# Gate logits of the first layer: eight dot products per token tile on VectorE in place of transposes and products on TensorE

## The chip, the cores and the metric

The kernel runs on one core of one Trainium2 chip. The metric is the device time in microseconds (us) from launch to end; for each kernel the median of several runs is given, and one more run is profiled. A core has several engines that work side by side and wait for one another on semaphores: TensorE (PE in the profile, with its weight loads as PEld), VectorE (DVE), ScalarE (ACT), GpSimd (POOL) and SyncE (SP, which here only issues DMA transfers).

## The reference

Two layers run one after the other over 2708 tokens (rows) of 256 numbers. Each has a masked attention, then a layer of eight experts of which every token uses two. Cut to what matters here, and with the shapes in brackets, layer 0 is:

```python
x = x + elu(softmax(where(adj > 0, q @ k.T / 16, -9e15)) @ v)   # q, k, v from layernorm(x)
xt = layernorm(x)                                # [2708, 256]
logits = xt @ Wr + br                            # [2708, 8]: the gate
probs = softmax(logits)
top_p, top_idx = top_k(probs, 2)
weights = top_p / top_p.sum(axis=-1)
xn = (xt - mean(xt)) / sqrt(var(xt) + 1e-5)      # normed a second time
# expert e: gelu((xn * ln_g[e] + ln_b[e]) @ W1[e] + b1[e]) @ W2[e] + b2[e]
x = x + sum of the two chosen experts' outputs, by weights
```

Layer 1 has another attention and another eight experts with the same top two; the change touches only the gate of layer 0. Since `xt` is `(x - mean) * once`, where `once` is one factor per token, the logits without bias are `once` times the dot of `x` with the gate's column less that column's mean over the 256 rows.

## The kernel before, in words

**Tiles.** Tokens go in 22 tiles of 128 rows (the last has 20), a tile's rows on the 128 partitions. Queries are worked on in six blocks of 512 (the last has 148 queries, tiles 20 and 21 being its two; the 512-query blocks hold four tiles each).

**Attention of layer 0** (`layer0_attention`). Each block goes over the 22 key tiles, one key step `k` each: `scores` (L545, products of 128x512 into the PSUM tile `s`, which has two buffers), the exponential on ACT (L557), the mask on DVE (L560, a multiplication by 0 or 1), and `attend` (L609, four products into the PSUM tiles `acc`), which runs three key steps behind its scores (`LAG`). At the ends of blocks the last columns' masks come in through small products (L552, with `apart` made by DVE in L432) and comparisons (L564, L595). While block b runs, DVE builds the masks of block b+1 out of `adj` (L411, L417), into the tile `mT`; after a block its masks are written to DRAM for layer 1 (`neighbours<-mT`).

**Routing.** When a block ends, `evict` copies its `acc` to `raw` (L634) and puts one sequence of steps for each tile on a `Line`: a new tile begins every three key steps, and every key step moves each begun tile on to its next `yield`. The sequence is `finish` (L297 to L302, L617 to L628: division by the sum, elu with ACT's exponential in L622, addition of x) and then `Experts.route`:

- `norm_stats`: mean and variance (L251, L252), then factors `once` and `twice` by a power on POOL (L257);
- `xt`, the row normed once (L261, the group xn<-x), and the row normed twice (L261, row<-x), which is copied (L1143), since a row is sent to two experts;
- `to_columns`: two transposes of `xt` on PE (L274) and a copy by ACT to `gT` (L275);
- two products of `gT` with the gate `wr` (L1156, four records in the trace for a tile), and the bias added by DVE (L1160);
- top two (L1167, L1168), exponential (L1185), the choice as zeros and ones in `sel` (L1183), each row's place by two small products (L1188, L1189) and some DVE work (L1192 to L1204), and two indirect DMAs by POOL (L1207), which send the rows to `disp`.

Tiles 0 to 15 go this way in blocks 1 to 4, 16 and 17 in block 5, and 18 to 21 in the first slots of the experts that follow. In block 1, one step of `fold_gate` every four key steps prepares weights of layer 1; it begins with two dots on DVE (L212) over `wdst_b`, one of the constants loaded at the start.

**Experts of layer 0** (FFN0, `slots`). Each slot takes 128 rows of one expert: columns of the rows (L1429, L1435), up products (L1457), gelu on ACT (L1465), down products (L1473), scaling by DVE (L1479), and addition to the token's row by an indirect DMA of POOL (L1492).

**Order.** SP's transfers are issued in the order written. The instructions of the other engines are put in order by a scheduler that works on its own estimates, so a change in one place can move instructions in others; the engines then run their orders strictly. Layer 1 has orders written by hand.

Of the kernel before, what the change touches and what calls it, by code (L numbers as in the profile page):

```python
# [9 lines left out]
F32 = mybir.dt.float32  # L10
I32 = mybir.dt.int32
# [9 lines left out]
P = 128  # L21
# [83 lines left out]
def adj_ffn_kernel(ctx: ExitStack, tc: tile.TileContext, a: dict, out: bass.AP):  # L105
# [81 lines left out]
    gb_b = load_bcast("L1_ffn_gate_b", E)  # L187
    bfc_b = load_bcast("L1_gnn_b_fc", D)

    wdst_b = load_bcast("L1_gnn_w_att", D, D)  # L190

    def load_dmajor(pool, name, n):
        t = pool.tile([P, DC, n], F32, name=f"{name}_w")
        nc.sync.dma_start(t, a[name].rearrange("(c p) n -> p c n", p=P))
        return t

    wr = const.tile([P, DC, E], F32, name="wr")
    wg = const.tile([P, DC, E], F32, name="wg")


    wfc = const.tile([P, DC, VALUES + 1 + E], F32, name="wfc")

    bfc_gate = const.tile([P, E], F32, name="bfc_gate")
    for to, name in ((wr, "L0_ffn_Wr"), (wg, "L1_ffn_gate_w"), (wfc[:, :, :D], "L1_gnn_W_fc")):
        constants.append(
            partial(nc.sync.dma_start, to, a[name].rearrange("(c p) n -> p c n", p=P))
        )

    def fold_gate():
        for c in range(DC):  # L210
            junk = small.tile([P, D], F32, name="junk", bufs=1)
# [4 lines left out]
        share = routing.tile([P, DC, P], F32, name="gT", bufs=2)  # L216
# [12 lines left out]
        def times_gate(dst, src):  # L229

            turned = routing.tile([P, DC, P], F32, name="gT", bufs=2)
            to_columns(turned, src, P)
            ps = misc.tile([P, GROUP, P], F32, name="misc").rearrange("p g n -> p (g n)")
            for c in range(DC):
                nc.tensor.matmul(
                    ps[:, :E], turned[:, c], G[:, c], start=(c == 0), stop=(c == DC - 1)
                )
            nc.vector.tensor_copy(dst, ps[:, :E])

        for c in range(DC):  # L240
            times_gate(wfc[:, c, D:VALUES], wfc[:, c, :D])
            yield
        times_gate(bfc_gate, bfc_b)


    def norm_stats(src, r):

# [105 lines left out]
    def layer0_attention(line):  # L353
        with ExitStack() as scope, ExitStack() as until_last:
# [114 lines left out]
                    )  # L469
                nc.scalar.copy(v[:r, t, :D], ps[:r, :D])  # L470

            with tc.tile_pool(name="fold", bufs=1, side="right") as fold:
                wq = load_dmajor(fold, "L0_gnn_Wq", D)
                wk = load_dmajor(fold, "L0_gnn_Wk", D)
                load_x(0)
                load_x(1)
                wv = load_dmajor(wide, "L0_gnn_Wv", D)
                for t in range(2, 9):
                    load_x(t)

                with tc.manual_schedule(
                    engines={mybir.EngineType.DVE, mybir.EngineType.Pool}
                ):
                    begun = [norm_begin(t) for t in range(2)]
                    first = []
                    for t in range(2, 4):
                        first.append(norm_end(*begun.pop(0)))
                        begun.append(norm_begin(t))
                    first.extend(norm_end(*x) for x in begun)
                    mT = mask_of(0)  # L490
                    first_mask = masks_of(0, mT)
                    for _ in range(GROUP):
                        next(first_mask)
                for start in constants:
                    start()

                flat = []
                for w in (wq, wk):
                    f = fold.tile([P, DC, D], F32, name=f"flat{len(flat)}")
# [145 lines left out]
            folding = fold_gate()  # L645
            for b, (b0, nb, ts_) in enumerate(BLOCKS):
                later_mask = iter(())
                if b + 1 < len(BLOCKS):
# [2 lines left out]
                for k in range(NT):  # L651
# [384 lines left out]
        return packed, hc, w2, b2, b1, ln, row  # L1036

    class Experts:
        def __init__(self, layer, hidden, packed_weights, w_gate, gate_bias, own_norm, xd, disp, early):
            self.hidden, self.packed_weights, self.own_norm = hidden, packed_weights, own_norm  # L1040
            self.w_gate, self.gate_bias, self.xd, self.disp = w_gate, gate_bias, xd, disp

            self.seen = const.tile([P, E], BF16, name=f"seen{layer}")
            nc.vector.memset(self.seen, 0.0)
# [59 lines left out]
        def route(self, t, x, logits=None):  # L1104


            own_norm, xd, disp, seen = self.own_norm, self.xd, self.disp, self.seen
            w_gate, gate_bias = self.w_gate, self.gate_bias
            r = ROWS[t]
            if own_norm:  # L1110
                rows2 = routing.tile([P, 2, DROW], F32, name="row")
            else:
                rows2 = kept_pool.tile([P, 2, DROW], F32, name="row", bufs=6)
            mean, once, twice, _ = norm_stats(x[:r], r)
            yield
            if not own_norm:

# [2 lines left out]
                self.beside_early(nc.sync.dma_start(of_tile(xd, t), x[:r]))  # L1120

            if own_norm:
                xt = rows.tile([P, D], F32, name="xn", bufs=4)[:r]
                normed(xt, x[:r], mean, once)
                normed(by_quarters(rows2[:r, 0, :D]), in_chunks(x[:r]), mean, twice)
            else:
                row = normed(by_quarters(rows2[:r, 0, :D]), in_chunks(x[:r]), mean, once)
# [4 lines left out]
            else:  # L1132
# [7 lines left out]
                    reason="no sooner than the row",  # L1140
                )
            if own_norm:
                nc.vector.tensor_copy(rows2[:r, 1, :D], rows2[:r, 0, :D])  # L1143
            yield
            if not own_norm:
                (nc.vector.tensor_copy if self.begun else nc.scalar.copy)(
                    rows2[:r, 1, :D], rows2[:r, 0, :D]
                )
            lg = small.tile([P, E], F32, name="lg")
            if logits is None:  # L1150
                gT = routing.tile([P, DC, P], F32, name="gT", bufs=2)
                to_columns(gT[:, :, :r], xt, r)
                yield
                ps = misc.tile([P, GROUP, P], F32, name="misc").rearrange("p g n -> p (g n)")
                for c in range(DC):
                    nc.tensor.matmul(  # L1156
                        ps[:r, :E], gT[:, c, :r], w_gate[:, c, :],
                        start=(c == 0), stop=(c == DC - 1),
                    )
# [426 lines left out]
    experts0 = Experts(0, 1024, packed0, wr, br_b, True, xd0, disps[0], 16)  # L1586
    experts1 = Experts(1, 512, packed1, wg, gb_b, False, xd1, disps[1], 14)

    neighbours = [
        dram.tile([P, m.width], FP8, name=f"neighbours{b}") for b, m in enumerate(MASKS)  # L1590
# [77 lines left out]
```

## Time and profile before

| | |
|---|---|
| three runs | 1214.02, 1209.07, 1212.79 us; median 1212.79 |
| profiled execution | 1217.16 us, of which the span of the page 1215.5 |
| mean granted TensorE clock | 0.982 |
| before block 1 (0 to 112 us) | PE busy 101.0, DVE 63.1 |
| blocks 1 to 5 (112 to 501 us) | PE busy 383.9, DVE 215.5 |
| experts of layer 0 (501 to 816 us) | PE busy 313.6, DVE 87.5 |
| layer 1 and the end (816 to 1215 us) | PE busy 347.0, DVE 200.1 |

In a profile line for a group of instructions stand the source line, the engine, the operation, the tiles it writes and reads with their shapes, and a count; then the busy time in us and the mean time of one in ns; then the idle time of the engine ahead of them and what ended it. Busy times of PE overlap between records, so differences of starts are the better measure of what an instruction holds the engine. In a line of the timeline the start comes first, then the duration in us. A line of waits names who waited for whom, then the total, the number of times and the longest.

### The profile page before, as it was taken

Reading aid. Unit: us, or ns where it says so; the run is one execution under the profiler, and the core shown is the slowest. Engines: PE = TensorE matmul, PEld = TensorE weight load, DVE = VectorE, ACT = ScalarE, POOL = GpSimd, SP = SyncE. Lnnn points to the kernel's source line nnn. Section 1 sums busy time; section 2 is a strip of 40 time slices with the busy share of each in tenths; the row PEclk is TensorE's granted clock in tenths of the full one; section 3 lists DMA queues with packets and bytes.
Section 4 is the critical chain, followed back from the end, with each engine's and each line's share of the span. In section 5 each row is a group of like instructions: output and inputs, shape, how many; then the busy total and the mean of one; then the engine's idle time right before and its main releaser. Section 6 shows DMA issues by size and latency. Waiting matters only on the chain. (4 is left out here: it accounts for less than half of the span.)

```text
span 1215.5 us, 20794 instructions
## 1 busy us (share of the span) xinstructions
PE 1145.4 (94%) x6512; PEld 924.1 (76%) x6512; DVE 566.2 (47%) x2147; ACT 431.9 (36%) x1252; POOL 416.0 (34%) x519
## 2 busy tenths in 40 slices
PE   8989999999998999999999999998999988899990
PEld 5666666666665666789999999996999977789880
DVE  5466663754645647452222222224866776322224
ACT  3222221221212222353333333333776747444440
POOL 3011021110211213253333343334645558555540
PEclk9999999999998999899999999999999999999996
DMA  9394962999969394847677955633002427555557
GB/s 200 58 181 76 194 160 88 226 209 267 221 133 219 83 192 164 276 102 219 174 222 228 352 118 154 179 95 100 1 1 76 178 62 209 168 139 132 170 179 282
DMA packets 199628, 197.11 MB, mean 162 GB/s; under 512 B 91403, under 2 KB 183012, under 8 KB 193368
## 3 DMA queue, kind: packets, MB, share of 16 engines
q1 hardware_dynamic: 172442, 109.39, 40.6%
q0 software_dynamic: 26176, 83.56, 21.8%
q10 hardware_dynamic: 894, 2.77, 0.6%
q8 instruction: 54, 0.88, 0.3%
q14 instruction: 62, 0.51, 0.1%
HBM read 252.62 MB, written 66.15 MB: 262 GB/s over the span
## 5 line engine op out<-in xcount | busy, mean ns | idle before, releaser
L1457 PEld LDWEIGHTS mm<-xe,ring 128*128 128x128 f32 x2192 | 259.7, 194 | 26.0 <-issue 11.7
L1457 PE MATMUL mm<-xe,ring 128*128 128x128 f32 x2192 | 265.6, 278 | 14.5 <-DMA ring<-L_ffn_packed,weight_row 7.1
L1473 PE MATMUL acc<-ring,hT 128*128 128x256 f32 x1096 | 254.3, 381 | 1.1 <-issue 1.1
L1465 ACT ACTIVATE hT<-mm,ring 128x128 f32<-128x128 f32 x548 | 156.6, 370 | 273.1 <-issue 168.1
L1473 PEld LDWEIGHTS acc<-ring,hT 128*128 128x128 f32 x1096 | 201.3, 191 | 26.0 <-issue 2.3
L609 PEld LDWEIGHTS acc<-v,p 128*128 128x128 f32 (+1 forms) x880 | 159.7, 190 | 65.2 <-issue 41.0
L609 PE MATMUL acc<-v,p 128*128 128x257 f32 (+1 forms) x880 | 204.6, 384 | 2.3 <-DVE p L560 1.3
L545 PE MATMUL s<-g,xnT 128*128 128x512 f32 x420 | 203.0, 603 | 0.0
L1479 DVE SCALAR_TENSOR_TENSOR y<-acc,who,bias 128x256 f32<-128x256 f32 x92 | 44.4, 482 | 339.2 <-PE acc L1473 322.9
L257 POOL TENSOR_TENSOR ln_rs<-ln_rs,minus_half 128x2 f32<-128x2 f32 x88 | 66.0, 752 | 252.0 <-DVE ln_rs L253 214.4
L1207 POOL DMA_INDIRECT disp<-row,to x88 | 90.4, 1027 | 166.2 <-DVE to L1204 58.2
L1368 POOL DMA_INDIRECT ring<-L_ffn_packed,weight_row x92 | 97.6, 1060 | 128.3 <-PE acc L1473 88.4
L557 ACT ACTIVATE p<-s 128x512 f32<-128x512 f32 x105 | 62.5, 596 | 181.4 <-PE s L545 143.0
L854 PE MATMUL acc<-parts,m 128*128 128x266 f32 x924 | 126.2, 293 | 0.0
L854 PEld LDWEIGHTS acc<-parts,m 128*128 128x128 f32 x924 | 117.1, 185 | 4.1 <-ACT raw L881 0.9
L545 PEld LDWEIGHTS s<-g,xnT 128*128 128x128 f32 x420 | 76.6, 192 | 53.8 <-issue 50.5
L560 DVE SCALAR_TENSOR_TENSOR p<-p,mT 128x512 f32<-128x512 f32 x100 | 68.4, 686 | 95.2 <-ACT p L557 93.6
L1492 POOL DMA_INDIRECT xd<-y,who x45 | 71.8, 1595 | 118.7 <-issue 70.4
L821 ACT CAST m<-mT 128x512 fp32r<-128x512 fp8e4 (+4 forms) x168 | 71.6, 475 | 11.4 <-PE acc L854 7.0
L1485 POOL DMA_INDIRECT xd<-y,who x47 | 47.1, 1002 | 23.6 <-issue 11.0
L411 DVE TENSOR_SCALAR m_rows<-adj 128x512 fp8e4<-128x512 int32 (+1 forms) x105 | 42.1, 432 | 2.0 <-DMA adj<-in_adj_dram 1.9
L417 DVE STREAM_TRANSPOSE mT<-m_rows 128x128 int32<-128x128 int32 x100 | 33.4, 393 | 0.1
(252 smaller groups left out, 1028.3 us busy)
## 6 DMA issues: line engine op xcount, KB each, us to landing
adj<-in_adj_dram SPq DMA_DIRECT2D x100, 256.0 KB
L_ffn_packed<-in_L_ffn_W_dram SPq DMA_DIRECT2D x16, 1024.0 KB
xg<-disp SPq DMA_DIRECT2D x368, 32.0 KB
L_ffn_packed<-in_L_ffn_W_dram SPq DMA_DIRECT2D x16, 512.0 KB
neighbours<-mT SPq DMA_DIRECT2D x5, 1408.0 KB
mT<-neighbours SPq DMA_DIRECT2D x5, 1408.0 KB
xin<-in_x_dram SPq DMA_DIRECT2D x42, 128.0 KB
ring<-L_ffn_packed SPq DMA_DIRECT2D x4, 1154.0 KB
```

The source lines that it names most:

```text
L257: nc.gpsimd.tensor_tensor(rs[:r, 1], rs[:r, 0], minus_half[:r], ALU.pow)
L545: nc.tensor.matmul(ps[:kr, :nb], xnT[:, c, k0 : k0 + kr], g[:, c, :nb], start=(c == 0), stop=(c == DC - 1 and k < KEYS),)
L560: nc.vector.scalar_tensor_tensor(p, p, LARGEST, mask, op0=ALU.min, op1=ALU.mult)
L609: nc.tensor.matmul(accs[j][:r], p[keys, q0 : q0 + r], v[keys, k, :], start=(k == 0), stop=(k == NT - 1),)
L821: nc.scalar.copy(m[:, : q1 - q0], MASKS[b].of_key(mTs[b], k)[:, q0 - b * BN : q1 - b * BN],)
L854: nc.tensor.matmul(acc[:r], masks[t], parts[:, k, i], start=(k == 0 and i == 0), stop=False,)
L1207: nc.gpsimd.indirect_dma_start(disp[:], bass.IndirectOffsetOnAxis(ap=to[:r, j : j + 1], axis=0), rows2[:r, j], None,)
L1368: nc.gpsimd.indirect_dma_start(w, None, packed[:], bass.IndirectOffsetOnAxis(ap=self.weight_row[:, s : s + 1], axis=0), bounds_check=E * P ...
L1457: nc.tensor.matmul(ps[:, i, :], w[:, c * hidden + f * P : c * hidden + (f + 1) * P], xe[:, c, :], start=(c == 0), stop=(c == DC - 1),)
L1465: nc.scalar.activation(hT[:, f, :], ps[:, i, :], AF.Gelu, bias=w[:, b1 + f : b1 + f + 1])
L1473: nc.tensor.matmul(ps, hT[:, f, :], w[:, w2 + f * D : w2 + (f + 1) * D], start=(f == 0), stop=(f == hc - 1),)
L1492: start = nc.gpsimd.indirect_dma_start(xd[:], at, y, None, bounds_check=N - 1, oob_is_err=False, compute_op=ALU.add)
```

## The change

For layer 0 the row `xt`, its transposes, the copy to `gT`, the products and the addition of the bias out of PSUM are gone. In their place stand eight multiplications with accumulation on DVE for a tile (`gate_dots`), each of which leaves one logit per token: four behind the statistics and four behind the copied row. They read the row before normalisation, and `wr_rows`, which holds the eight gate columns, less their means, as rows on all 128 partitions. The elementwise products are written to the second half of the tile `rows2` and are overwritten by the copied row. The factor `once` and the bias are then applied in one instruction. `wr_rows` is made at the end of block 0 (`gate_rows`): a broadcast load into a buffer of `adj`, a sum on DVE, and a subtraction on POOL. One `yield` in `route` goes, since there is no product to wait for.

Some tiles move as well: `wr` is gone; `wdst_b` is loaded in `fold_gate` at the beginning of block 1 and no longer at the start; it, `junk` and `gT` of `fold_gate` come from the pool `wide`; and the weights of the first stage lie in a buffer of `mT`. The small writes of padding rows to `disp` are issued by SP two row fetches earlier.

```diff
-    wdst_b = load_bcast("L1_gnn_w_att", D, D)
...
-    wr = const.tile([P, DC, E], F32, name="wr")
+    wr_rows = rows0.tile([P, E, D], F32, name="wr_rows", bufs=1)
...
-    def fold_gate():
+    def fold_gate(pool):
+        wdst_b = pool.tile([P, D], F32, name="wdst_b", bufs=1)
+        nc.sync.dma_start(wdst_b, a["L1_gnn_w_att"][D : 2 * D].partition_broadcast(P))
...
+    def gate_rows(raw):
+
+        raw = raw.rearrange("p (d e) -> p d e", e=E)
+        mean = small.tile([P, E], F32, name="gate_mean", bufs=1)
+        nc.vector.tensor_reduce(mean, raw.rearrange("p d e -> p e d"), AX.X, ALU.add)
+        nc.vector.tensor_scalar(mean, mean, 1.0 / D, None, ALU.mult)
+        nc.gpsimd.tensor_tensor(
+            wr_rows, raw.rearrange("p d e -> p e d"),
+            mean.unsqueeze(2).to_broadcast([P, E, D]), ALU.subtract,
+        )
+
+    def gate_dots(lg, x, r, experts, unused):
+
+        for e in experts:
+            nc.vector.scalar_tensor_tensor(
+                unused, x, 1.0, wr_rows[:r, e],
+                op0=ALU.mult, op1=ALU.mult, accum_out=lg[:r, e : e + 1],
+            )
...
+                    if b == 0 and k == NT - 4:
+                        raw = wide.tile([P, BN // QUARTER, P], I32, name="adj", bufs=3)
+                        raw = raw.rearrange("p n e -> p (n e)").bitcast(F32)
+                        nc.sync.dma_start(
+                            raw, a["L0_ffn_Wr"].rearrange("d e -> (d e)").partition_broadcast(P)
+                        )
+                        gate_rows(raw)
...
             mean, once, twice, _ = norm_stats(x[:r], r)
+            lg = small.tile([P, E], F32, name="lg")
+            if own_norm:
+                dots = small.tile([P, E], F32, name="dots")
+                gate_dots(dots, x[:r], r, range(E // 2), rows2[:r, 1, :D])
+                logits = dots[:r]
             yield
...
             if own_norm:
-                xt = rows.tile([P, D], F32, name="xn", bufs=4)[:r]
-                normed(xt, x[:r], mean, once)
                 normed(by_quarters(rows2[:r, 0, :D]), in_chunks(x[:r]), mean, twice)
...
             if own_norm:
+                gate_dots(dots, x[:r], r, range(E // 2, E), rows2[:r, 1, :D])
                 nc.vector.tensor_copy(rows2[:r, 1, :D], rows2[:r, 0, :D])
             yield
...
-            lg = small.tile([P, E], F32, name="lg")
-            if logits is None:
-                gT = routing.tile([P, DC, P], F32, name="gT", bufs=2)
-                to_columns(gT[:, :, :r], xt, r)
-                yield
-                ps = misc.tile([P, GROUP, P], F32, name="misc").rearrange("p g n -> p (g n)")
-                for c in range(DC):
-                    nc.tensor.matmul(
-                        ps[:r, :E], gT[:, c, :r], w_gate[:, c, :],
-                        start=(c == 0), stop=(c == DC - 1),
-                    )
-                nc.vector.tensor_add(lg[:r], ps[:r, :E], gate_bias[:r])
-            else:
-                nc.vector.scalar_tensor_tensor(
-                    lg[:r], logits, once, gate_bias[:r], op0=ALU.mult, op1=ALU.add
-                )
+            nc.vector.scalar_tensor_tensor(
+                lg[:r], logits, once, gate_bias[:r], op0=ALU.mult, op1=ALU.add
+            )
```

More of the change, by code (lines that the diff above doesn't have):

```diff
@@ L188, in adj_ffn_kernel, with load_dmajor @@
     bfc_b = load_bcast("L1_gnn_b_fc", D)
-    wdst_b = load_bcast("L1_gnn_w_att", D, D)
-    def load_dmajor(pool, name, n):
-        t = pool.tile([P, DC, n], F32, name=f"{name}_w")
+    def load_dmajor(t, name):
         nc.sync.dma_start(t, a[name].rearrange("(c p) n -> p c n", p=P))
         return t
-    wr = const.tile([P, DC, E], F32, name="wr")
+    wr_rows = rows0.tile([P, E, D], F32, name="wr_rows", bufs=1)
     wg = const.tile([P, DC, E], F32, name="wg")
@@ L203, in adj_ffn_kernel @@
     bfc_gate = const.tile([P, E], F32, name="bfc_gate")
-    for to, name in ((wr, "L0_ffn_Wr"), (wg, "L1_ffn_gate_w"), (wfc[:, :, :D], "L1_gnn_W_fc")):
+    for to, name in ((wg, "L1_ffn_gate_w"), (wfc[:, :, :D], "L1_gnn_W_fc")):
         constants.append(
@@ L207, in adj_ffn_kernel @@
         )
-    def fold_gate():
+    def fold_gate(pool):
+        wdst_b = pool.tile([P, D], F32, name="wdst_b", bufs=1)
+        nc.sync.dma_start(wdst_b, a["L1_gnn_w_att"][D : 2 * D].partition_broadcast(P))
         for c in range(DC):
-            junk = small.tile([P, D], F32, name="junk", bufs=1)
+            junk = pool.tile([P, D], F32, name="junk", bufs=1)
             nc.vector.scalar_tensor_tensor(
@@ L215, in fold_gate @@
             )
-        share = routing.tile([P, DC, P], F32, name="gT", bufs=2)
+        share = pool.tile([P, DC, P], F32, name="gT", bufs=2)
         nc.gpsimd.memset(share[:, 0], 1.0 / D)
@@ L229, in times_gate @@
         def times_gate(dst, src):
-            turned = routing.tile([P, DC, P], F32, name="gT", bufs=2)
+            turned = pool.tile([P, DC, P], F32, name="gT", bufs=2)
             to_columns(turned, src, P)
@@ L470, in prepare @@
                 nc.scalar.copy(v[:r, t, :D], ps[:r, :D])
-            with tc.tile_pool(name="fold", bufs=1, side="right") as fold:
-                wq = load_dmajor(fold, "L0_gnn_Wq", D)
-                wk = load_dmajor(fold, "L0_gnn_Wk", D)
+            fold = wide.tile([P, MASKS[0].width], FP8, name="mT", bufs=3)
+            fold = fold[:, : 16 * DC * D].bitcast(F32).rearrange("p (i c n) -> p i c n", i=4, c=DC)
+            if True:
+                wq = load_dmajor(fold[:, 0], "L0_gnn_Wq")
+                wk = load_dmajor(fold[:, 1], "L0_gnn_Wk")
                 load_x(0)
                 load_x(1)
-                wv = load_dmajor(wide, "L0_gnn_Wv", D)
+                wv = load_dmajor(wide.tile([P, DC, D], F32, name="wv"), "L0_gnn_Wv")
                 for t in range(2, 9):
@@ L498, in layer0_attention @@
                 for w in (wq, wk):
-                    f = fold.tile([P, DC, D], F32, name=f"flat{len(flat)}")
+                    f = fold[:, 2 + len(flat)]
                     for o in range(DC):
@@ L644, in layer0_attention @@
             late, total, accs, apart = [], None, None, None
-            folding = fold_gate()
+            folding = fold_gate(wide)
             for b, (b0, nb, ts_) in enumerate(BLOCKS):
@@ L1038, in adj_ffn_kernel, with __init__ @@
     class Experts:
-        def __init__(self, layer, hidden, packed_weights, w_gate, gate_bias, own_norm, xd, disp, early):
+        def __init__(self, layer, hidden, packed_weights, gate_bias, own_norm, xd, disp, early):
             self.hidden, self.packed_weights, self.own_norm = hidden, packed_weights, own_norm
-            self.w_gate, self.gate_bias, self.xd, self.disp = w_gate, gate_bias, xd, disp
+            self.gate_bias, self.xd, self.disp = gate_bias, xd, disp
             self.seen = const.tile([P, E], BF16, name=f"seen{layer}")
@@ L1107, in route @@
             own_norm, xd, disp, seen = self.own_norm, self.xd, self.disp, self.seen
-            w_gate, gate_bias = self.w_gate, self.gate_bias
+            gate_bias = self.gate_bias
             r = ROWS[t]
@@ L1585, in adj_ffn_kernel @@
     packed1 = pack_weights("L1_ffn", 512, False)
-    experts0 = Experts(0, 1024, packed0, wr, br_b, True, xd0, disps[0], 16)
-    experts1 = Experts(1, 512, packed1, wg, gb_b, False, xd1, disps[1], 14)
+    experts0 = Experts(0, 1024, packed0, br_b, True, xd0, disps[0], 16)
+    experts1 = Experts(1, 512, packed1, gb_b, False, xd1, disps[1], 14)
     neighbours = [
```

## The prediction

> **What bounds the kernel now.** The page first: its top, the busy shares, and the groups of a key step.
>
> ```profile
> span 1215.5 us, 20794 instructions
> PE 1145.4 (94%) x6512; PEld 924.1 (76%) x6512; DVE 566.2 (47%) x2147; ACT 431.9 (36%) x1252; POOL 416.0 (34%) x519
> L545 PE MATMUL s<-g,xnT 128*128 128x512 f32 x420 | 203.0, 603 | 0.0
> L560 DVE SCALAR_TENSOR_TENSOR p<-p,mT 128x512 f32<-128x512 f32 x100 | 68.4, 686 | 95.2 <-ACT p L557 93.6
> ```
>
> PE is the bound, and DVE is half idle. But the change works in one stage, so next the windows of the stretches in which layer 0 routes: query block 2, the handover to FFN0, and 4 us of it.
>
> ```profile
> 204.00:290.00 86.00, 86.00 (x359) 57.00 (x358) 45.31 (x165) 18.42 (x42) 12.72 (x21) 1.00 1.06 223
> 501.00:536.00 35.00, 33.55 (x219) 31.00 (x220) 21.15 (x111) 20.98 (x54) 14.89 (x18) 0.90 0.48 117
> 502.00:506.00 4.00, 4.00 (x20) 4.00 (x20) 2.44 (x16) 0.67 (x3) 0.00 (x0) 0.50 0.76 215
> ```
>
> After the time come PE, PEld, DVE, ACT, POOL, then PE's granted clock. In block 2 PE is full at full clock, DVE has 41 us free. At the handover the clock is halved. Then PE's waits from 112 to 536 us:
>
> ```profile
> PE s L552 <- DVE apart L432: 3.0, 1, 3.0
> PE misc L274 <- DVE xn L261: 1.5, 3, 0.8
> PE acc L609 <- ACT p L557: 1.0, 2, 0.5
> PE mm L1457 <- ACT raw L634: 1.0, 1, 1.0
> ```
>
> Few and small: PE time removed here comes off the end, as long as DVE stays on time. Last the timeline around one routed tile and at the handover:
>
> ```profile
> 160.16 0.51 PE L1156 MATMUL misc<-wr,gT 128*128 128x8 f32 x4
> 160.52 1.96 PE L545 MATMUL s<-g,xnT 128*128 128x512 f32 x4
> 167.56 0.42 PE L274 MATMUL misc<-ident,xn 128*128 128x128 f32 x2
> 500.19 0.43 DVE L634 COPY raw<-acc 128x257 f32<-128x257 f32 x1 [3.14 <-PE acc L609]
> 501.12 0.34 DVE L1435 TENSOR_SCALAR xe<-xe_raw,ring 128x128 f32<-128x128 f32 x1
> 501.67 1.10 PE L1457 MATMUL mm<-xe,ring 128*128 128x128 f32 x4 [0.98 <-ACT raw L634]
> ```
>
> **PE work removed.** Starts are what PE spends, since matmuls overlap. The transposes of a tile hold PE for 0.25 us (167.56 to the next start, 167.81), the products 0.36 (160.16 to 160.52), and the score product behind them takes 1.80 instead of 1.72 (162.32 less 160.52): 0.69 per tile. Sixteen tiles go through blocks 1 to 4: 11.0 us. Tiles 16 and 17 (block 5, 1.6) and 18 to 21 (first FFN0 slots, 3.1 and 0.8 of waiting) are in the handover sum below.
>
> **DVE work added.** The exact form of a dot is already in the timeline:
>
> ```profile
> ```
>
> The first starts at 36.01, its read at 36.35, the second at 36.47: 0.46 us a dot, 3.7 a tile, less one normalising that goes (L261, 0.33 from start to start). Four tiles a block add 13.4 us of DVE to 41 us free: over a block it fits. What counts is bursts, since the dots stand in DVE's fixed order among the masks (L560) that feed attend (L609). I summed the start-to-start times of DVE's instructions between successive masks in the new order, against the 3.45 us of a key step. Block 1: 4.5, 3.9, 3.6, 4.4, 5.5, 3.4, 4.1, 3.4, 4.1, 4.4, 1.8. With what stands before them DVE falls behind by up to 6.3 us there, 4.3, 3.6 and 4.3 in blocks 2 to 4 (by 1.4 in block 1 before). Against that: a mask is done at 127.6 and its attend starts near 135.4, three key steps on, so 7.8 us of slack; ACT, which waits for DVE in `finish` (L622) with the next score behind it, has two score buffers in PSUM: two key steps less 1.72 of product and 0.60 of exp (L557), some 4.5 us. Only block 1 is past the second. From nothing (all inside the slack) to the 18.5 us of the four peaks (no slack at all), I take 1.5, being near the covered end: only 6.3 - 4.5 = 1.8 is uncovered.
>
> [...]
>
> **The stall on `apart`** (3.0 us, end of block 3). L432 stands behind the block's routing on DVE. By the same sum DVE reaches it 13.7 to 14.8 us after a point from which PE takes 11.95 with the products gone: a stall of 1.7 to 2.8. I take 2.3: -0.7. Its half clock (0.50 over 378 to 382) stays.
>
> **The handover.** Tile 16's rank product and a late mask cost block 5 about 1.5 and 1.3 us of waiting, against 1.6 of PE work gone: last attend at 501.6 instead of 500.7 (a key step is 1.68 us there, and single steps hold up to five dots). Then, in DVE's new order, some 30 instructions (row, lg, top-2, sel, weights of tiles 17 to 19, with trips to ACT and PE) stand between the eviction (L634) and the first expert columns (L1435), which before came 0.93 us after it (500.19 to 501.12). Their start-to-start times and the trips sum to 4.98, and 6.0 to the second chunk: the first up product (L1457) starts at 506.2 instead of 501.67, +4.5. The 16 dots of tiles 20 and 21 stand ahead of the second expert slot's columns; PE reaches tile 20's rank product near 523.6, finds it 3.4 us late, but has 3.9 us of products, transposes and waiting less. Counted through, the third slot's up products start at 531.8 instead of 528.8: net +3.0 for the whole handover, block 5 included. From 0 (the order costs nothing, the slots' own slack takes it) to 6.
>
> **New idle on PE and the clock.** A lapse to half clock costs about 3.4 us: after the 3.02 us idle at 375.56, eight score products took 5.63 instead of 3.44, and the rest follows to 386. The one at 502 exists before. A second, at the late slot or in block 5, is likely, not certain: 0 to 6.8, I take 3.0.
>
> **Covered, taken at nothing.** The gate rows' load (8 KB to each of 128 partitions) goes to an `adj` buffer free by 115 us; first needed at 139. The DVE sum over 128x2048 (2.3 us if it goes on from 320 ns at 128x160 and 404 at 128x240, both L1267; half as much again if it is slowed as the turned L1244 is, 478 ns against 319 for L1280) lies in DVE's idle stretches at 122.7 to 126.9. POOL's subtraction of 128x2048 is eight of L764's 754 ns, 6.0 us, to 12 if its strided read doubles it; POOL is idle from 111.4 to 140.8 but for one memset. The weights of `fold_gate` (L212) are now loaded behind the 1.4 MB `neighbours` write, which took 6 us from 122.4; they land near 129 to 130, and DVE waits for them with the second mask of block 1 (130.36) behind it: up to 1 us late, inside the 7.8. If POOL's end lies past 139, or the loads land 5 us later, this cover is gone and block 1 stands still for the difference, up to 6 us. ACT's copy of 372 ns and DVE's wait for L1156 (8.7 us) go too; nothing ended on either.
>
> A dot takes 420 ns, a 128x256 operation of one source 282 (L621). [...]
>
> **Sum.** -11.0 (products and transposes) -0.7 (apart) +1.5 (lag) +3.0 (handover) +3.0 (clock) = -4.2. The profiled execution took 1217.16 (span 1215.5), 4.4 above the median of 1212.79; it becomes 1213.0, and the median 1208.6, rounded to 1209.
>
> **Rivals.** *All of it covered (faster).* The lag stays inside the slack and no new half clock comes: -11.0 - 0.7 + 3.0 = -8.7, 1204. For: only 13.4 of 41 us are asked for, and 1.29 us of idle once left the clock alone. Against: the burst of 6.3 and the clock at 502. Its far end, with no wait at the handover either (then -11.0 - 1.6 - 3.9 = -16.5), is 1196.
>
> *DVE becomes the bound in bursts (slower).* If DVE is later than the slack in blocks 1 to 4, as when each dot costs more than its row or ACT's 4.5 us is really less, PE stalls in every block, and each stall may halve its clock. It decides from about 3 us less slack: then the peaks leave 4.8, 2.8, 2.1 and 2.8, together 12.5, of which I take 10.5 since DVE catches up while PE stands, and two lapses more than forecast (6.8): -4.2 - 1.5 + 10.5 + 6.8 = +11.6, 1224. For: the new order holds up to five dots, 2.3 us, between two masks. Against: 7.8 us of mask slack.
>
> *The gate rows or the late weights are late (about the same).* The setup stands at the head of DVE's queue in block 1: -4.2 + 4 is no gain, 1213; 1215 at its 6 us.
>
> That the change leaves the work on PE can be excluded: the transposes and products of layer 0 are gone from PE's order.
>
> **Numbers.** 0.5% is 6.1 us, about what a measurement of this kernel tells from no change: faster is under 1206.7, slower over 1218.9. Forecast 0.46 (its own spread 1202 to 1215: 0.15 faster, 0.30 same, 0.01 slower), covered 0.24 (faster), bursts 0.23 (0.21 slower, 0.02 same), setup 0.07 (0.05 same, 0.02 slower): 0.39, 0.37, 0.24. The range: leaving 0.08 below and 0.12 above, 1198 to 1224.
>
> **What would show it.** After: no L1156, and L274 without 42 transposes; PE waits in blocks 1 to 4 of 2 us at most; `apart` near 2.3; first L1457 4 to 5 us after the last eviction; dots of 420 ns, 0.46 apart. Wrong if L609 or L545 waits for DVE or ACT by several us in each block (bursts), if DVE waits at the fold weights or dots (setup), or if the clock in block 2 is under 0.97.

## The result and the profile after

| | before | changed |
|---|---|---|
| median, 7 runs each | 1212.34 us | 1223.82 us |
| lowest to highest | 1204.50 to 1214.99 | 1219.99 to 1226.14 |
| profiled execution | 1217.16 (span 1215.5) | 1225.38 (span 1223.7) |
| mean granted TensorE clock | 0.982 | 0.971 |

The ratio of the medians is 1.0101, with a 95% interval of 1.0072 to 1.0130: slower by 11.5 us where 4 us less had been forecast. The profiled executions differ by 8.2 us.

The top of the page after, and the groups of scores, masks and dots:

```profile
span 1223.7 us, 20834 instructions
PE 1136.5 (93%) x6380; PEld 915.5 (75%) x6380; DVE 618.3 (51%) x2479; ACT 423.9 (35%) x1230; POOL 425.1 (35%) x520
L566 PE MATMUL s<-g,xnT 128*128 128x512 f32 x420 | 202.4, 602 | 0.6 <-ACT p L578 0.5
L581 DVE SCALAR_TENSOR_TENSOR p<-p,mT 128x512 f32<-128x512 f32 x100 | 72.6, 728 | 57.2 <-ACT p L578 56.9
```

The work is what the diff says: 132 matmul records fewer, and PE is busy 8.9 us less. Yet the end is 8.2 us later: what PE was spared came back as idling and more. The same three stretches as before tell where (length, then busy time of PE, PEld, DVE, ACT and POOL, then the clock, the DMA share and GB/s):

```profile
204.00:290.00 86.00, 84.90 (x322) 54.12 (x321) 53.15 (x226) 17.51 (x39) 13.55 (x23) 1.00 1.08 227
501.00:536.00 35.00, 22.56 (x145) 20.83 (x145) 23.63 (x142) 14.17 (x37) 14.45 (x17) 0.80 0.32 77
502.00:506.00 4.00, 0.00 (x0) 0.00 (x0) 0.00 (x0) 0.00 (x0) 0.00 (x0) 0.50 0.66 218
```

Block 2 is as full as before, at full clock, with DVE busy 7.8 us longer and nothing waiting for it. At the handover PE is busy 22.6 of 35 us instead of 33.6, and from 502 to 506 us no compute engine has any work at all: no engine is short of time there, all of them wait for a transfer. PE's waits from 100 to 560 us name the place (total, times, longest):

```profile
PE misc L1207 <- DVE sel L1202: 15.6, 4, 10.0
PE s L566 <- ACT p_last L578: 5.9, 2, 5.6
PE s L573 <- DVE apart L451: 2.8, 1, 2.8
PE acc L630 <- ACT p L578: 1.0, 2, 0.5
```

The last two lines stood there before in nearly the same size (3.0 and 1.0); the first two are new. Both lead to DVE, and DVE's own waits from 440 to 520 us say what it stood for:

```profile
DVE xe_raw L1448 <- DMA xg<-disp: 8.1, 1, 8.1
DVE apart_last L451 <- DMA adj_rest<-in_adj_dram: 7.0, 1, 7.0
DVE apart L451 <- DMA adj_rest<-in_adj_dram: 4.9, 1, 4.9
```

Three waits for transfers, against none before: 8.1 us at the handover, 7.0 us in block 5, and 4.9 us near the end of block 4. The third held up no product of block 4, as PE's waits show, and it is still there (5.2 us) in a_late below, where the other two are gone; so the first two are followed here. The timeline shows the first of them between the last eviction and the first up product:

```profile
497.37 0.43 DVE L655 COPY raw<-acc 128x257 f32<-128x257 f32 x1 [4.65 <-PE acc L630]
506.63 0.45 DVE L1448 STREAM_TRANSPOSE xe_raw<-xg 128x256 f32<-128x256 f32 x1 [8.10 <-DMA xg<-disp]
507.86 0.17 PE L1207 MATMUL misc<-sel,before 128*128 128x8 bf16 x1 [9.99 <-DVE sel L1202]
510.68 1.62 PE L1476 MATMUL mm<-xe,ring 128*128 128x128 f32 x6 [0.60 <-DMA who<-disp]
```

The eviction comes at 497.37, 2.8 us earlier than before; the first up product at 510.68, 9.0 us later.

A ledger by stages, between the starts of the first eviction copies of the blocks (L634 before, L655 after) and from the last of them to the start of the third slot's `y` (L1479, L1498), carries the rest of this text. It gives lengths in us, each from the one profiled execution of its kernel:

| kernel | blocks 1, 2, 3, 4 | block 5 | last eviction to third slot's `y` | span |
|---|---|---|---|---|
| before | 83.5 81.7 88.3 75.7 | 37.1 | 33.7 | 1215.5 |
| changed | 80.8 80.3 86.0 72.5 | 44.1 | 45.4 | 1223.7 |

Blocks 1 to 4 gain 9.5 us. Block 5 loses 7.0 and the handover 11.7, together 18.7.

### The profile page after: what moved, and what is told of

Read it like the earlier page. It is cut to its first block, busy times and chain, and to the rows that moved or that the text cites. A ratio compares the mean times of both kernels' runs of the same rounds, so it can differ in the third digit from the quotient of the medians.

```text
span 1223.7 us, 20834 instructions
## 1 busy us (share of the span) xinstructions
PE 1136.5 (93%) x6380; PEld 915.5 (75%) x6380; DVE 618.3 (51%) x2479; ACT 423.9 (35%) x1230; POOL 425.1 (35%) x520
## 5 line engine op out<-in xcount | busy, mean ns | idle before, releaser
L1476 PEld LDWEIGHTS mm<-xe,ring 128*128 128x128 f32 x2192 | 262.4, 195 | 23.6 <-issue 12.0
L1498 DVE SCALAR_TENSOR_TENSOR y<-acc,who,bias 128x256 f32<-128x256 f32 x92 | 44.4, 482 | 343.2 <-PE acc L1492 343.2
L1226 POOL DMA_INDIRECT disp<-row,to x88 | 91.2, 1036 | 161.0 <-DVE to L1223 33.7
L581 DVE SCALAR_TENSOR_TENSOR p<-p,mT 128x512 f32<-128x512 f32 x100 | 72.6, 728 | 57.2 <-ACT p L578 56.9
L260 DVE SCALAR_TENSOR_TENSOR row<-x,wr_rows 128x256 f32<-128x256 f32 (+1 forms) x176 | 72.0, 415 | 0.4
```

Of the source, the lines that this page charges most:

```text
L260: nc.vector.scalar_tensor_tensor(unused, x, 1.0, wr_rows[:r, e], op0=ALU.mult, op1=ALU.mult, accum_out=lg[:r, e : e + 1],)
L581: nc.vector.scalar_tensor_tensor(p, p, LARGEST, mask, op0=ALU.min, op1=ALU.mult)
L1226: nc.gpsimd.indirect_dma_start(disp[:], bass.IndirectOffsetOnAxis(ap=to[:r, j : j + 1], axis=0), rows2[:r, j], None,)
L1476: nc.tensor.matmul(ps[:, i, :], w[:, c * hidden + f * P : c * hidden + (f + 1) * P], xe[:, c, :], start=(c == 0), stop=(c == DC - 1),)
```

## The experiments

Ratios are against runs of the kernel before on the same chip, with 95% intervals. Theories at the outset: the dots that DVE does at the handover cost the time (the prediction's own step, undersized); or a dependency that the dots have nothing to do with; and for block 5, a transfer that is no earlier although PE is.

**Memory overlap.** In the memory map of the built program, the tiles of the FFN0 slots begin 752 bytes inside the memory that layer 0's attention still holds, where the last block's masks lie; before they began above it. `wr_rows`, 8 KB a partition, lives on beside the routed rows and takes the room. (The bytes are the map's; the runs show the wait that comes and goes with them.) The first `xe_raw` therefore waits until the last masks have been read by their write to DRAM (`neighbours<-mT_last`). a_mt1 gives up two buffers that are never used and so removes the overlap alone; b_pad brings one into the kernel before.

a_mt1, in the changed kernel:

```diff
-                mT = of_block(b, "mT", [P, MASKS[b].width], FP8, bufs=3)
+                mT = of_block(b, "mT", [P, MASKS[b].width], FP8, bufs=3 if b < last else 1)
```

> Changed kernel, with one buffer instead of three for the last block's mask tile, of which only one is ever used: 7 KB of the attention's memory go, so that the experts' tiles no longer lie over it. Theory memory (the first expert columns wait for the write of the last mask, since their pool overlaps the attention's): the 8.1 us wait at xe_raw is gone, the first up product starts about 2 to 5 us after the last eviction instead of 13.3, and the total falls by 8 to 10 us, to about 1214-1216. Theory order (some 30 routing instructions on DVE hold the columns back): the first product still starts about 10 us or more after the eviction, total within 3 us of the changed kernel. The 7.0 us wait of DVE for adj_rest in block 5 stays in both.

Measured: 1219.78 us, 1.0025 [1.0008, 1.0042]. The wait of `xe_raw` is gone, and the transpose stands straight behind the eviction, as before the change:

```profile
494.76 0.43 DVE L655 COPY raw<-acc 128x257 f32<-128x257 f32 x1 [4.66 <-PE acc L630]
495.10 0.43 DVE L1448 STREAM_TRANSPOSE xe_raw<-xg 128x256 f32<-128x256 f32 x1
496.70 0.68 PE L1476 MATMUL mm<-xe,ring 128*128 128x128 f32 x4 [1.44 <-issue]
```

The first up product comes 1.9 us after the eviction (13.3 in the changed kernel), and the handover takes 39.8 instead of 45.4. DVE's order is the same as in the changed kernel up to the last eviction and differs from there: part of what the edit gives is the order that the scheduler makes without the dependency.

b_pad, in the kernel before:

```diff
-                bias2 = two.tile([P, D], F32, name="bias2", bufs=2 if own_norm else 4)
+                bias2 = two.tile([P, D], F32, name="bias2", bufs=6 if own_norm else 4)
```

> Kernel before, with six instead of two buffers for the experts' bias tile, so that the experts' pool reaches 656 bytes into the attention's memory; nothing of the change is in it. Theory memory: the first expert columns now wait for the write of the last mask, issued at 508 us in the kernel before: the first up product starts near 511-513 instead of 501.7, total +9 to +12 us (about 1222). Theory order: no change, within 3 us of the kernel before.

Measured: 1231.78 us, 1.0124 [1.0102, 1.0145]. Without a single dot, 656 bytes of overlap cost 15 us, more than the 9 to 12 expected, with the same wait:

```profile
DVE xe_raw L1429 <- DMA xg<-disp: 9.4, 1, 9.4
```

The profile calls it `xg<-disp`, but the rows of `xg` had long been there. What ended it was the write of the masks, on whose semaphore the built program lets this `xe_raw` wait. SP's issues and the transposes show it:

```profile
503.35 0.40 SPq L722 DMA_DIRECT2D neighbours<-mT_last  x1
506.63 0.45 DVE L1448 STREAM_TRANSPOSE xe_raw<-xg 128x256 f32<-128x256 f32 x1 [8.10 <-DMA xg<-disp]
```

```profile
507.97 0.40 SPq L694 DMA_DIRECT2D neighbours<-mT_last  x1
511.02 0.45 DVE L1429 STREAM_TRANSPOSE xe_raw<-xg 128x256 f32<-128x256 f32 x1 [9.43 <-DMA xg<-disp]
```

The first pair is the changed kernel, the second b_pad: 3.28 and 3.05 us from issue to transpose. In the kernel before the same issue came at 508.09, 7.6 us after `xe_raw` (500.53): no dependency there.

**Block 5: the load of `adj_rest`.** a_rest issues the last block's `adj_rest` early in block 4, into a second buffer; a_both adds a_mt1's edit; b_rest is a_rest's edit in the kernel before, as a control.

```diff
-                adj = wide.tile([P, GROUP, REST], I32, name="adj_rest", bufs=1)
+                adj = wide.tile([P, GROUP, REST], I32, name="adj_rest", bufs=2)
...
+                    if b == last - 1 and k == 5:
+                        rest_last = load_rest(last)
```

> Changed kernel, with the last block's adj_rest loaded in block 4 (key step 5, a second buffer) instead of behind the last masks' write. Theory transfers (PE came 10 us early to block 5, but the queue of transfers did not): the 7.0 us wait of DVE and PE's 5.6 us go, block 5 ends about 7 us earlier, and the total falls by 6 to 9 us if the wait of the first expert columns for the mask's write moves forward with it, by 0 to 3 if that write is bound by the weights' loads. Theory dots (block 5 is late because DVE has too much to do there): the eviction of block 5 moves by less than 2 us.

> Both edits. The order of instructions is the one of the adj_rest edit alone; only the waits for the attention's memory are gone. If the two stalls are all that the change lost: about 1206 to 1209, below the kernel before by 3 to 6 us. If the DVE order of the handover is what costs, about 1213 or more.

> Kernel before with adj_rest loaded in block 4: a control of that edit without the change. DVE does not wait for this load in the kernel before, so every theory expects no change, within 2 us.

Measured: a_rest 1222.02, 1.0057 [1.0038, 1.0076]; a_both 1219.17, 1.0022 [1.0005, 1.0038]; b_rest 1224.87, 1.0070 [1.0047, 1.0094]. DVE's wait for `adj_rest` in block 5 goes, but block 5 falls only to 41.5 and 41.0, between what the two theories of a_rest expected, and a_both is no better than a_mt1 and far from the 1206 to 1209 expected if the two stalls were all. The control, which was to change nothing, says why this can't be read: alone in the kernel before, the edit costs some 8.5 us, since the scheduler answers with another order at the handover (first up product 7.3 us after the eviction instead of 1.5). These three settle little about `adj_rest`.

"late" is an edit that moves nothing but SP's order: the copy of the last expert's weights into `L_ffn_packed` is issued behind the masks' write and `adj_rest`. In the traces the orders of PE, DVE, ACT and POOL are the same with and without it, up to 560 us. a_late is a_mt1's edit and this one, b_late this one alone in the kernel before, o_late this one alone in the changed kernel.

```diff
-                    if background and b > 0 and k % 5 == 1 and (b > 1 or k > 10):
+                    if background and b > 0 and k % 5 == 1 and (b > 1 or k > 10) and (b != last - 1 or k < 20):
```

> The changed kernel without the overlap of memory, dots for all tiles, and the last weights behind adj_rest. Theory transfers: block 5 falls from 41.5 to 37-39 us and the total by 3 to 5 us against the run without the overlap, to a ratio of 0.998 to 1.000; what is left against the 16-tile run (6 to 7 us) is the dots at the handover.

> Kernel before with the last weights behind adj_rest: control. DVE does not wait for adj_rest there, so every theory expects no change, within 2 us.

> The changed kernel as it is, overlap of memory included, with only the last weights moved behind adj_rest in SP's order; no other engine's order moves. If the wait for adj_rest and the wait for the last mask's write are two losses of their own that add: block 5 falls from 44.2 to 37 or 38 us, the wait at xe_raw stays at 8 us or more, and the ratio is about 1.005 (1.003 to 1.007). If the second wait only follows the first: the wait at xe_raw shrinks to under 4 us and the ratio is near 0.9975, that of the run with both removed. If the second wait takes up what the first gives back (the mask's write stays where the experts' weights let it): xe_raw waits 13 us or more and the ratio stays at 1.008 to 1.012.

Measured: b_late 1217.05, 0.9996 [0.9982, 1.0011], a neutral control. a_late 1213.75, 0.9975 [0.9963, 0.9987]; o_late 1224.11, 1.0039 [1.0017, 1.0062]. In both, block 5 is back, at 37.4 and 37.1 us, and DVE's wait for `adj_rest` in it is 0.2 us and none; o_late keeps the wait of the overlap:

```profile
DVE xe_raw L1448 <- DMA xg<-disp: 8.5, 1, 8.5
```

With the changed kernel and a_mt1 this makes a square of four: 1.0101 with both losses, 1.0039 without block 5's, 1.0025 without the overlap, 0.9975 with neither. The overlap is worth 0.0064 or 0.0076 (7.8 or 9.2 us), block 5 0.0050 or 0.0062 (6.1 or 7.5 us), whichever is taken first: within the intervals, they add. Block 5 and handover together (89.6 us in the changed kernel, 86.3 in o_late, 81.3 in a_mt1, 77.3 in a_late) say the same of the overlap, 8.3 or 9.1 us, but give only 3.2 or 4.0 for block 5: with the overlap the handover grew by 3.8 when block 5 shrank, and a_mt1, whose engines have the changed kernel's orders there, needed 41.5 us for block 5 with a wait of 4.3 instead of 7.0. So the cause of block 5's loss is shown, and its worth lies between 3 and 7.5 us. a_late has neither loss, as the prediction's sum had neither, and it is about 3 us faster than before, where 4.2 had been forecast.

**The dots by themselves.** b_dots adds the eight dots per tile to the kernel before (on a constant row, results unused), while the transposes and products stay:

```diff
+                    nc.vector.scalar_tensor_tensor(
+                        rows2[:r, 1, :D], x[:r], 1.0, bv_b[:r],
+                        op0=ALU.mult, op1=ALU.mult, accum_out=dots[:r, e : e + 1],
+                    )
```

> Kernel before with eight dots per tile added on DVE at the places where the change has them, by a constant row, their results unused: the cost of the dots alone, with no work taken from PE. Blocks 1 to 4 keep their lengths within 1 us each if the slack of 7.8 and 4.5 us covers the bursts. Theory DVE at the handover: block 5 grows by 4 to 7 us, the third slot ends 5 to 7 us later after the eviction, total +9 to +13. Rival (dots are covered in block 5 too, losses are memory and transfers alone): total within 3 us of the kernel before.

Measured: 1232.92, 1.0142 [1.0112, 1.0171], more than either expectation. Blocks 85.4, 81.9, 88.1, 75.3: four tiles of dots a block cost 1.9 us in block 1 and nothing that stands out of ±0.4 in the others. Block 5 takes 0.6 more and not 4 to 7, the handover 45.7 instead of 33.7: +12.0. The dots are free where DVE has room. The 12.0 are not theirs alone: the scheduler put the first `xe_raw` 6.0 us behind the eviction here, behind routing, and b_rest, which has a like order and not one dot more, takes 38.8 for its handover, 5.1 more than before.

**Dots for tiles 0 to 15 only.** In h16_mt1 tiles 16 to 21 go by transposes and products, with a_mt1's edit; h16_both adds a_rest's, h16_late the "late" order. h18_late has dots up to tile 17.

```diff
+            by_dots = own_norm and t < 16
...
+                if not by_dots:
+                    xt = rows.tile([P, D], F32, name="xn", bufs=4)[:r]
+                    normed(xt, x[:r], mean, once)
```

> Changed kernel with one buffer for the last mask tile (no overlap of memory), and with the dots for tiles 0 to 15 only: tiles 16 to 21, routed in block 5 and in the first expert slots, take transposes and products as before. Theory DVE at the handover (what the change still loses without the overlap is the dots of six tiles on DVE where a key step is 1.7 us and the experts' columns wait): block 5 falls from 41.5 to 37-39.5 us, the third expert slot ends 33.7 to 35 us after the last eviction instead of 39.8, the 9.5 us of blocks 1 to 4 stay, and the total is 7 to 9 us below the kernel before. Rival (PE 10 us early only waits for transfers, whose queue is not faster): block 5 stays over 41 us, total within 3 us of the kernel before.

> The same, and adj_rest loaded in block 4. If the load of adj_rest still binds with DVE relieved: block 5 is 2 to 4 us shorter than in the run without this edit and the total 2 to 4 us lower. If not: the same within 2 us.

> The run with dots for tiles 0 to 15 and no overlap of memory, and SP issues the copy of the last expert's weights (1 MB, block 4, key step 21) behind the masks' write and adj_rest instead of ahead of them. Nothing else moves on any engine. Theory transfers (block 5 is late since PE came early to a load that stands behind the queue's backlog): DVE's wait for adj_rest falls from 4.4 to under 1 us, PE's 3.1 us stall and the half clock behind it go, block 5 falls from 44.1 to 37 or 38 us, and the total by 5 to 7 us, to a ratio of 0.991 or 0.992. Rival (the wait is replaced by the next one, as with the early load): block 5 stays over 40 us.

> The same, with dots for tiles 16 and 17 (routed in block 5) as well. Theory handover (what dots cost is in the expert slots, where the columns wait for DVE): within 2 us of the run with 16 tiles. Rival (DVE cannot take the dots at 1.7 us a key step): block 5 grows by 3 us or more.

| kernel | blocks 1, 2, 3, 4 | block 5 | handover | time; ratio |
|---|---|---|---|---|
| a_mt1 | 80.8 80.3 86.0 72.4 | 41.5 | 39.8 | 1219.78; 1.0025 |
| a_late | 80.8 80.4 83.6 72.8 | 37.4 | 39.9 | 1213.75; 0.9975 |
| o_late | 80.8 80.4 86.0 73.6 | 37.1 | 49.3 | 1224.11; 1.0039 |
| h16_mt1 | 80.8 80.3 85.2 72.4 | 44.1 | 33.0 | 1213.15; 0.9971 [0.9948, 0.9993] |
| h16_both | 80.8 80.3 86.7 72.4 | 40.5 | 38.5 | 1216.30; 1.0011 [0.9998, 1.0024] |
| h18_late | 80.8 80.3 85.3 72.4 | 36.3 | 38.4 | 1212.84; 0.9966 [0.9948, 0.9983] |
| h16_late | 80.8 80.3 83.6 72.9 | 37.0 | 34.3 | 1207.63; 0.9919 [0.9897, 0.9940] |

h16_mt1 brings the handover back to the length before, while block 5 stays at 44.1 with no dot in it: that loss is not the dots'. The expectation that block 5 would fall with them missed, the rival held, and the total came 3.0 us below the kernel before instead of 7 to 9. The clock is halved in block 5, over 460 to 468 us, as in the changed kernel (0.57):

```profile
460.00:468.00 8.00, 7.37 (x23) 4.59 (x23) 6.34 (x33) 2.04 (x9) 1.80 (x4) 0.50 0.06 18
```

h16_late mends that, as expected, and beats both kernels, at 9.6 us less than before on its chip. Its handover (last eviction at 488.8) is as full as the one before the change, where PE was busy 33.55 of 35 us at a clock of 0.90:

```profile
489.80:524.80 35.00, 33.46 (x217) 30.70 (x218) 20.63 (x109) 21.03 (x53) 14.42 (x18) 0.90 0.49 121
```

h18_late missed its expectation: the dots of tiles 16 and 17 cost block 5 nothing (36.3), but the handover became 38.4 without one dot in it: the scheduler put a slot's `xe_raw` ahead, where it waits 5.0 us for its rows. h16_both carries the disturbed order of a_rest's edit.

## Why the prediction was right or wrong

The term that failed is the handover's: +3.0 us, block 5 included, and +3.0 more for one new lapse of the clock. Measured were +7.0 in block 5 and +11.7 at the handover. That a new lapse would follow gaps of a few us was the author's estimate, since no run shows how long a gap has to be; the one that came in block 5 (0.57 over 460 to 468 us) went with 5.56 us of idle on PE. The rest of the sum held.

**Blocks 1 to 4: right.** Forecast were -11.0 for products and transposes, -0.7 for the `apart` stall and +1.5 of lag, together -10.2; measured -2.6, -1.4, -2.3, -3.2, together -9.5. The `apart` stall is 2.8 us, at the late end of the 1.7 to 2.8 given for it, so it gave 0.2 and not 0.7, and its half clock stayed (0.50 over 370 to 374 us). PE's small waits for DVE and ACT there, `sel` 1.1, `p` 1.0 and 0.5, come to 2.6 us, of which 1.0, that of `acc`, was already there before: what is new is close to the lag term. DVE did not become the bound in bursts, so that rival fell; that its 1224, the upper end of the range, is the time measured is chance. The gate rows cost nothing either: block 1 gained 2.6 us, and nothing on PE waited for them. That DVE's sum took 3.79 us against at most 3.5 estimated, and POOL's subtraction 4.72 against at least 6.0, changed nothing.

A dot was priced by the one at the start of the kernel before:

```profile
36.01 0.42 DVE L212 SCALAR_TENSOR_TENSOR junk<-wfc,L_gnn_w_att_b 128x256 f32<-128x256 f32 x1
36.35 0.08 DVE L212 DVE_READ_ACCUMULATOR junk<-wfc,L_gnn_w_att_b 128x1 f32 x1
36.47 0.42 DVE L212 SCALAR_TENSOR_TENSOR junk<-wfc,L_gnn_w_att_b 128x256 f32<-128x256 f32 x1
36.82 0.08 DVE L212 DVE_READ_ACCUMULATOR junk<-wfc,L_gnn_w_att_b 128x1 f32 x1
```

In the changed kernel a dot has the same duration:

```profile
L260 DVE SCALAR_TENSOR_TENSOR row<-x,wr_rows 128x256 f32<-128x256 f32 x168 | 69.2, 415 | 0.4
```

but the pitch of 0.46 was too much, because the scheduler mixes the dots with other instructions, and the read then starts with the next one:

```profile
139.32 0.41 DVE L260 SCALAR_TENSOR_TENSOR row<-x,wr_rows 128x256 f32<-128x256 f32 x1
139.65 0.08 DVE L260 DVE_READ_ACCUMULATOR row<-x,wr_rows 128x1 f32 x1
139.65 0.18 DVE L271 BATCH_NORM_AGGREGATE ln_mv<-ln_st 128x2 f32<-128x6 f32 x1
```

That is 0.33 us from start to start.

**Block 5: the step that failed is the cover taken for granted.** "PE time removed here comes off the end" was read from PE's waits before. It holds while the next thing that PE needs is as early as PE is. PE comes into block 5 9.8 us earlier (453.2 against 463.0), and meets a transfer that is not. Before, SP issued the masks' write at 456.15 and `adj_rest` behind it at 456.57, and the data were there when DVE reached them at 463.39. After:

```profile
446.37 0.60 SPq L1049 DMA_DIRECT2D L_ffn_packed<-in_L_ffn_W_dram  x1
449.32 0.53 SPq L722 DMA_DIRECT2D neighbours<-mT  x1
449.95 1.35 SPq L450 DMA_DIRECT2D adj_rest<-in_adj_dram  x2
460.64 0.31 DVE L451 TENSOR_SCALAR apart_last<-adj_rest 128x296 fp8e4<-128x296 int32 x1 [6.99 <-DMA adj_rest<-in_adj_dram]
```

Issued 6.6 us earlier, used only 2.8 us earlier: `adj_rest` stands behind 1.4 MB of masks and the last expert's weights, whose first copy went out at 446.37 here but at 443.45 before, when 13 us lay between. The transfers did not keep pace with PE: the DMA share was already 1.06 in block 2 in the prediction's own first window (1.08 after), and in the changed kernel it was 0.90 over 449.95 to 460.64 us, from the issue of `adj_rest` to its use. Instead of the +0.9 us by which block 5 was to end later, it took 7.0 more, and the clock lapsed in it. o_late, where only SP's order moves, shows the cause: with `adj_rest` ahead of the weights, block 5 takes 37.1 us.

**Handover: the memory overlap was in no step.** It costs 8.1 us of waiting here and was in none of the rivals, so the first up product came 13.3 us after the eviction. Nor was the step that stood in its place sound: the 4.98 us of some 30 DVE instructions between the eviction and the first columns was worked out of the changed kernel's order, and that order was itself the scheduler's answer to the dependency. With the overlap gone, the columns follow the eviction directly (a_mt1). An order that puts the rows' transpose far behind a step it stood next to calls for the question why.

**Handover: the dots were right in kind, and a little small.** In a_late, without overlap and without the wait in block 5, the handover takes 39.9 against 33.7: +6.2 us, where 2.1 of delay (3.0 with the 0.9 of block 5) and 3.0 of half clock, 5.1, had been forecast. The place is the one named: the 16 dots of tiles 20 and 21 hold up tile 20's rank product, by 3.4 us in the forecast and by 4.2 in a_late, where DVE does fourteen of them from 506.01 on before it comes to `sel`:

```profile
506.01 0.40 DVE L260 SCALAR_TENSOR_TENSOR row<-x,wr_rows 128x256 f32<-128x256 f32 x1
513.71 0.41 DVE L260 SCALAR_TENSOR_TENSOR row<-x,wr_rows 20x256 f32<-20x256 f32 x1
514.05 0.17 DVE L1202 TENSOR_TENSOR sel<-hot 128x8 bf16<-128x8 f32 x1
514.27 0.17 PE L1207 MATMUL misc<-sel,before 128*128 128x8 bf16 x1 [4.22 <-DVE sel L1202]
```

And h16_mt1 and h16_late, without these dots, have a handover of 33.0 and 34.3. The runs don't part the dots from the order that comes with them: h18_late loses 4 us there by its order alone.

**The sum.** -9.5 in blocks 1 to 4, +7.0 in block 5, +11.7 at the handover, of which a_late's 6.2 goes with the dots and their order and the remaining 5.5 with the overlap: +9.2, by the spans +8.2, by the medians +11.5. The profiled executions lie 4.8 us above the median before and 1.6 after, and layer 1, where nothing was changed, differs by up to 4 us between profiles, so the last 3 us are not resolved here.

## What to carry to other kernels

PE time saved ahead of a load is worth only what the load's arrival leaves of it (PE came into block 5 9.8 us earlier here, and block 5 took 7.0 more): read in SP's issues what stands ahead of the first transfer of the next stage, and whether it too gets earlier. A tile that lives past its stage can push the next stage's tiles onto memory that is still in use, so look in the memory map at what the next stage's first tiles lie on and whose last transfer they then wait for; a few hundred bytes cost 8 to 15 us here, and giving up two unused buffers was the cure. Added work belongs where its engine has room: the same dots were nearly free for tiles 0 to 15 (1.9 us in block 1 of b_dots) and went with 6 us at the handover.

## What the runs showed of the hardware

**A mask that DVE began beside a POOL operation of 4.72 us took 5.18 us.** In the changed kernel, the subtraction that makes `wr_rows` and that mask:

```profile
126.48 4.72 POOL L252 TENSOR_TENSOR wr_rows<-adj,gate_mean 128x2048 f32<-128x2048 f32 x1 [14.65 <-DVE gate_mean L251]
126.58 5.18 DVE L581 SCALAR_TENSOR_TENSOR p<-p,mT 128x512 f32<-128x512 f32 x1 [0.17 <-ACT p L578]
```

The mask took 5.18 us where its like takes 0.69 (the next one, at 132.49), and ended 0.56 us after the subtraction. PE waited for nothing there, since the mask slack of 7.8 us covered it, but the prediction had taken the subtraction for free by POOL's idleness alone. Why it took that long no run shows. Beside a shorter POOL operation in the same execution, of 0.69 us and two elements a partition, a dot that DVE began 0.17 us into it took 0.42 us, where the dots' mean is 0.415.

```profile
227.03 0.69 POOL L276 TENSOR_TENSOR ln_rs<-ln_rs,minus_half 128x2 f32<-128x2 f32 x1 [4.74 <-DVE ln_rs L272]
227.20 0.42 DVE L260 SCALAR_TENSOR_TENSOR row<-x,wr_rows 128x256 f32<-128x256 f32 x1
```

**Gaps of the same length on PE were followed by different clocks.** The `apart` stall at the end of block 3 is 2.8 us in the changed kernel and in a_late, but the clock behind it (370 to 374 us) was 0.50 in the changed kernel:

```profile
370.00:374.00 4.00, 3.65 (x6) 1.88 (x7) 0.89 (x2) 0.46 (x2) 0.00 (x0) 0.50 0.84 259
```

and 1.00 in a_late:

```profile
370.00:374.00 4.00, 3.98 (x10) 1.87 (x11) 1.49 (x3) 0.66 (x2) 0.00 (x0) 1.00 1.02 254
```

Block 3 took 86.0 and 83.6 us, so this lapse was worth 2.4 us, where the prediction had priced one at 3.4. In the kernel before, the longer gap was not the one with the half clock either: behind 0.98 us of idle at 501.67 it was 0.50 over 502 to 506 us, behind 1.29 and 0.80 us of idle at 67.51 and 69.01 it was 1.00:

```profile
67.51 0.70 PE L609 MATMUL acc<-v,p 128*128 128x257 f32 x2 [1.29 <-DVE p L560]
69.01 0.41 PE L274 MATMUL misc<-ident,xn 128*128 128x128 f32 x2 [0.80 <-DVE ln_mv L252]
67.50:71.40 3.90, 2.68 (x10) 1.47 (x11) 2.78 (x9) 0.72 (x2) 1.70 (x2) 1.00 1.20 212
```
